# A four-layer graph network on one core: 46 instead of 42 target blocks of layer 3 from its table, and layer 0's table made first

## The chip, the core and the metric

The kernel runs on one core of a Trainium2 chip. The core has five engines that work side by side, each through its own queue in order: TensorE (PE; its weight loads, PEld, overlap its matmuls), VectorE (DVE), ScalarE (ACT), GpSimd (POOL) and SyncE (SP), which here only issues transfers. The metric is the time of the one core in microseconds (us), as the median of several runs.

## What is computed

There are 12,500 nodes of 128 features and 212,500 directed edges, sorted by target (a random graph in both directions, and a loop at each node). Four layers follow each other; each adds its result to x:

```
h = relu(layernorm(x));  x += L0(h)    # attention: Wh[src], 4 heads, softmax over a target's edges, gelu, layernorm
h = relu(layernorm(x));  x += L1(h)    # sum over edges of h[src] * edge_weight1, gelu, @W.T + b, gelu
h = relu(layernorm(x));  x += L2(h)    # h[src] mixed with 9 edge features, summed by target
h = relu(layernorm(x));  x += L3(h)    # mean of h[src] by target @Wl.T + b, + h@Wr.T, batch norm over nodes
```

In each layer the costly part is the same: fetch the row of each edge's source, and add the rows up by target.

## The kernel before

**Blocks and groups.** Nodes come in 98 blocks of 128 (`NB`), handled four at a time in 25 batches (`NBK`, `NK`). Edges come in 208 groups of 1,024 (`NG`, `GE`), eight slots of 128. As edges are sorted by target, a group's targets lie within a window of 128 nodes.

**Two ways to sum by target.** *By gather:* a group's source rows are fetched by eight indirect transfers that POOL issues (`gather`, line 661, and `gather_apart`, line 669), a one-hot matrix of the targets is made, and eight matmuls add the rows into the window, which DVE adds to the accumulator. *By table* (layers 1 and 3, `tabled1` and `tabled`): the layer's whole node table is held on chip (`tabS`). For each target block ("window", `NW` of them) the edges have been sorted by source block into 26 rows of 128 places (`NT`). A step takes one such row: four small matmuls pick the source rows out of `tabS` into `px` (lines 1200 and 1443), ACT copies and in layer 1 weights them, and one matmul scatters them to the window (`pw`, lines 1181 and 1429). What finds no place in its rows is gathered, one transfer for each window (`last`). Before the change blocks 56 to 97 (`W0_ = 56`, `NW = 42`) go by table in both layers, and the first `G0 = 121` groups by gather.

**Prologue.** The edges' targets and sources are loaded (`load_edges`, lines 128 to 138) and each group's base, relative targets (`rel`, stored again as `rel16`) and safety conditions worked out; small weights are loaded and transposed; then layer 0's table `tab0` (Wh and the source's part of the attention) and `sdt` (the target's part) are made in 25 batches (lines 917 to 952). Outside the layers' loops a list scheduler places the instructions on the engines by priority in the order of the source, as tiles and engines come free.

**Layer 0** (loop over `g`, lines 1093 to 1135, in the order written): loads for `g + 2`; the gathers and attention logits of `g` (`logits`, lines 992 to 1015); one-hot matrices on ACT (`hot`); every fourth group the softmax (`weights`, lines 1017 to 1063, scans on DVE); for group `g - 7` the messages (`spread_out`, line 1078, matmuls at 1082) and the addition to the accumulator (`add_up`, line 1086). 15 X buffers hold gathered rows. Beside this `Slots` (lines 750 to 916) sorts the edges of the 42 table blocks, three windows at a time (`quad`), mostly on DVE; its work is cut into steps: one `slots.step()` in each group and one more in every second (`slots.step(g % 2)`). A three takes 22 steps, so 14 threes take 308.

**Layer 3** (lines 1473 to 1566): group `g` is gathered into `xg` (28 buffers) while PE multiplies group `g - 1` into `pg` (line 1544, one PSUM buffer) and DVE reads `pg` of `g - 2` (lines 1536, 1537) and adds it up. From group 10 on, the table's steps are spread over the matmuls of the groups:

```
goal = total * (T * (g - first) + t + 1) // (T * (last_ - first + 1))
```

Finished batches go through `node3` (count, mean, two matrix products) and, at the end, `closing` (batch norm). Layer 1 is built likewise. Layer 2 goes by gather alone.

The functions that the change touches:

Of the kernel before, what the change touches and what calls it, by code (L numbers as in the profile page):

```python
# [14 lines left out]
F = mybir.dt.float32  # L15
# [11 lines left out]
P = 128  # L27
# [66 lines left out]
def gnn_kernel(ctx: ExitStack, tc, x, src, dst, ef16, ef9, ew, W0, We0, a0, lns, lnb, W1, b1,  # L94
# [11 lines left out]
    W0_ = NB * 56 // 98 // NBK * NBK  # L106
    NW = NB - W0_
    G0 = E * W0_ * P // (N * GE) + 2
# [88 lines left out]

    si = cst.tile([P, NG, T], I, name="si")
# [6 lines left out]
    early = ExitStack()  # L205
    tmp = early.enter_context(tc.tile_pool(name="acp", bufs=1))
    wslot = tmp.tile([P, NW, NT], F, name="wslot")
    bir = cst.tile([P, NG], I, name="bir")
    relx = cst.tile([P, GM, T], F, name="relx")
# [5 lines left out]
    NK = -(-NB // NBK)  # L215
# [5 lines left out]
    with tc.tile_pool(name="ed", bufs=1) as ep:  # L221
# [45 lines left out]
        last = base[:, G0 - GM : G0, None].to_broadcast([P, GM, T])  # L267
        vec.tensor_tensor(relx, rel[:, G0 - GM : G0, :], last, ALU.add)
        vec.tensor_scalar(relx, relx, W0_ * P - 0.5, 4.0 * P, op0=ALU.is_gt, op1=ALU.mult)
        vec.tensor_tensor(relx, relx, rel[:, G0 - GM : G0, :], ALU.add)  # L270
# [6 lines left out]
        vec.memset(least, 0.0)  # L277
        for k, g in enumerate(done):
            if g + 1 < NG:
                vec.memset(least[:, g + 1 :], float(min(NBK * P * (k + 1), N)))  # L280
        vec.memset(least[:, G0:], float(W0_ * P))
        for k, g in enumerate(done):
            if g + 1 >= G0 and g + 1 < NG:
                vec.memset(least[:, g + 1 :], float(min(NBK * P * (k + 1), N)))
# [3 lines left out]
        vec.memset(end, float(RW - W))  # L288
        for k, g in enumerate(done):
            if g + 6 < NG:  # L290
                vec.memset(end[:, g + 6 :], float(NBK * P * (k + 1) + RW - W))
# [27 lines left out]
        vec.tensor_scalar(many, red[:, 0, G0 - GM - 1 : G0 - GM], W0_ * P - 0.5, None, op0=ALU.is_gt)  # L319
        vec.scalar_tensor_tensor(worst, many, float(W), worst, op0=ALU.mult, op1=ALU.max)  # L320
# [17 lines left out]
    WE = cst.tile([P, P + 2 * H], F, name="WE")  # L338
# [3 lines left out]
    with tc.tile_pool(name="wt", bufs=2) as wp, tc.tile_pool(name="wtp", bufs=2, space=PSUM) as pp:  # L342
        for w, to in ((W0, WE[:, :P]), (W1, W1T), (Wl, WlT), (Wr, WrT)):
            wn = wp.tile([P, P], F, name="wn")
            nc.sync.dma_start(wn, w)
            wps = pp.tile([P, P], F, name="wps")
            pe.transpose(wps, wn, ident)
            vec.tensor_copy(to, wps)
            if w is W0:
                ab = wp.tile([P, 2 * H], F, name="ab", bufs=1)  # L350
                vec.memset(ab, 0.0)
                for h in range(H):
                    for s in range(2):
                        nc.sync.dma_start(ab[h * HD : (h + 1) * HD, s * H + h : s * H + h + 1],
                                          a0[h : h + 1, s * HD : (s + 1) * HD].rearrange("o d -> d o"))
                aps = pp.tile([P, 2 * H], F, name="aps", bufs=1)
                pe.matmul(aps, wn, ab, start=True, stop=True)
                vec.tensor_copy(WE[:, P:], aps)
# [67 lines left out]
    tab0 = dram.tile([N, P + H], F, name="tab0")  # L426
    sdt = dram.tile([AW, 3 * H], B16, name="sdt")
# [491 lines left out]
    WN = P + 2 * H  # L919
    with tc.tile_pool(name="p0", bufs=2) as sp, tc.tile_pool(name="p0p", bufs=2, space=PSUM) as pp:  # L920
        zs = sp.tile([P, 3 * H], B16, name="zs", bufs=1)
        vec.memset(zs, 0.0)
        for r in range(N, AW, P):
            n = min(P, AW - r)
            nc.sync.dma_start(sdt[r : r + n, :], zs[:n, :])
        for b0, nb in batches(4):
            xt = sp.tile([P, nb, D], F, name="xt")
            load_rows(xt, x, b0, nb)
            h = sp.tile([P, nb, D], F, name="h0")
            for _ in norm(sp, xt, nb, h):  # L930
                pass
            pt = pp.tile([P, nb, P], F, name="pt")
            for j in range(nb):
                pe.transpose(pt[:, j, :], h[:, j, :], ident)
            hT = sp.tile([P, nb, P], F, name="hT")
            act.copy(hT, pt)
            pw = pp.tile([P, 2, 512], F, name="pw")
            pwv = pw[:, :, : 2 * WN].rearrange("p a (c n) -> p a c n", n=WN)
            for j in range(nb):
                pe.matmul(pwv[:, j // 2, j % 2, :], hT[:, j, :], WE, start=True, stop=True)  # L940
            tt = sp.tile([P, nb, P + H], F, name="tt")
            sd = sp.tile([P, nb, H], F, name="sd")
            for a in range(0, nb, 2):
                act.copy(tt[:, a : a + 2, :], pwv[:, a // 2, : min(2, nb - a), : P + H])
                vec.tensor_copy(sd[:, a : a + 2, :], pwv[:, a // 2, : min(2, nb - a), P + H :])

            s3 = sp.tile([P, nb, 3, H], B16, name="s3")
            for k in range(3):
                vec.tensor_copy(s3[:, :, k, :], sd)
# [815 lines left out]
```

## Time and profile before

| | |
|---|---|
| median of 3 runs | 7448.18 us (7439.46 to 7453.02) |
| profiled execution: its own time, its span | 7429.66 us, 7427.8 us |
| mean granted TensorE clock | 0.789 of full |
| busy share of the span: PE, DVE, ACT, POOL | 68%, 71%, 38%, 69% |
| gathers on POOL: layers 0, 1, 2, 3 | 1,664, 968, 1,664, 968 |
| first and last gather of layer 0 | 231.9 and 2416.3 us |
| of layer 1 | 2524.9 and 3804.8 us |
| of layer 2 | 3900.5 and 5980.5 us |
| of layer 3 | 6016.7 and 7308.7 us |

The profile is of one execution. In its lines L661 is line 661 of the kernel before; a group of instructions is given as line, engine, operation, output<-input, count, then busy us and the mean ns of one, then the idle time of the engine just before them and what ended it ("issue": it waited for nothing that the profile shows). SPq is SP's transfer queue. A list of waits gives for each waiter and releaser the total us, the times and the longest one.

### The profile page before, as it was taken

Reading aid. Unit: us, or ns where it says so; the run is one execution under the profiler, and the core shown is the slowest. Engines: PE = TensorE matmul, PEld = TensorE weight load, DVE = VectorE, ACT = ScalarE, POOL = GpSimd, SP = SyncE. Lnnn points to the kernel's source line nnn. Section 1 sums busy time; section 2 is a strip of 40 time slices with the busy share of each in tenths; the row PEclk is TensorE's granted clock in tenths of the full one; section 3 lists DMA queues with packets and bytes.
Section 4 is the critical chain, followed back from the end, with each engine's and each line's share of the span. In section 5 each row is a group of like instructions: output and inputs, shape, how many; then the busy total and the mean of one; then the engine's idle time right before and its main releaser. Section 6 shows DMA issues by size and latency. Waiting matters only on the chain.

```text
span 7427.8 us, 119421 instructions
## 1 busy us (share of the span) xinstructions
PE 5056.1 (68%) x39957; PEld 3687.5 (50%) x39958; DVE 5283.1 (71%) x10506; ACT 2841.6 (38%) x7693; POOL 5145.2 (69%) x5372
## 2 busy tenths in 40 slices
PE   3344445444444499888987787778787758788787
PEld 2344444344444366555656777777777732222222
DVE  5678888888888445544448999999999944545454
ACT  1244444444444234434443333333333314444443
POOL 0577777777775377777737777777777767777772
PEclk8566666666666699999987888888888868888887
DMA  5444444444443433333322222222222244344333
GB/s 84 96 105 103 104 106 105 107 106 103 105 105 94 84 88 96 95 90 94 93 72 57 67 71 66 68 69 67 70 69 66 69 126 105 105 106 105 102 103 108
DMA packets 741279, 674.54 MB, mean 91 GB/s; under 512 B 341283, under 2 KB 629398, under 8 KB 740631
## 3 DMA queue, kind: packets, MB, share of 16 engines
q0 software_dynamic: 186624, 382.17, 21.4%
q1 hardware_dynamic: 554027, 284.63, 15.0%
q8 instruction: 316, 5.18, 0.3%
q14 instruction: 312, 2.56, 0.1%
HBM read 603.91 MB, written 63.28 MB: 90 GB/s over the span
## 4 chain that ended last, share of the span: by engine, by line
PE 26%; POOL 16%; DVE 10%; issue 9%; DMA 3%; ACT 1%; DVEq 1%; SPq 0%; POOLq 0%; ACTq 0%
POOL X L661 15%; PE pw L1181 5%; PE px L1200 5%; PE px L1443 4%; PE pw L1429 4%; PE pag L1275 3%; PE pg L1544 3%; DMA X<-htab,si 2%; DVE oh L680 1%; POOL X L669 1%; DVEq L692 1%; PE pag L1332 1%; DVE oh L676 1%; DVE f L1536 1%; DVE B L1314 1%
## 5 line engine op out<-in xcount | busy, mean ns | idle before, releaser
L661 POOL DMA_INDIRECT X<-tab,si x1664 | 1635.6, 983 | 531.0 <-issue 473.0
L661 POOL DMA_INDIRECT X<-htab,si x1664 | 1574.0, 946 | 533.7 <-issue 509.7
L669 POOL DMA_INDIRECT xg<-tab,si x968 | 919.7, 950 | 358.9 <-issue 127.3
L669 POOL DMA_INDIRECT X<-htab,si x968 | 937.1, 968 | 324.2 <-issue 83.8
L1082 PE MATMUL pag<-oh,msg 128*128 128x128 f32 x3328 | 670.5, 383 | 357.4 <-DVE msg L1078 328.7
L1082 PEld LDWEIGHTS pag<-oh,msg 128*128 128x128 f32 x3328 | 620.3, 288 | 373.7 <-DVE msg L1078 336.5
L1454 ACT CAST xb<-px 128x384 bf16<-128x384 f32 x1050 | 501.3, 478 | 737.4 <-PE px L1443 722.0
L1212 ACT ACTIVATE xs<-px,wslot 128x128 f32<-128x128 f32 x1050 | 382.6, 367 | 774.7 <-PE px L1200 698.2
L1332 PE MATMUL pag<-oh,A 128*128 128x128 f32 x3328 | 561.4, 341 | 0.0
L1544 PE MATMUL pg<-xg,oh 128*128 128x385 bf16 x968 | 370.9, 388 | 256.4 <-DVE f L1537 194.9
L1275 PE MATMUL pag<-oh,X 128*128 128x128 f32 x1936 | 432.6, 309 | 165.5 <-DVE acc L1268 121.6
L1332 PEld LDWEIGHTS pag<-oh,A 128*128 128x128 f32 x3328 | 543.5, 256 | 0.0
L1181 PE MATMUL pw<-ohb,xs 128*128 128x128 f32 x2100 | 541.3, 342 | 0.0
L1307 ACT ACTIVATE A<-X,ef 128x128 f32<-128x128 f32 x1664 | 509.9, 391 | 15.7 <-DMA X<-htab,si 15.4
L676 DVE TENSOR_TENSOR oh<-iop,rel 128x1024 f32<-128x1024 f32 (+1 forms) x321 | 388.7, 1211 | 163.2 <-PE pg L1544 162.7
L1200 PE MATMUL px<-tabS,oha 128*32 128x128 f32 x8652 | 488.1, 299 | 5.8 <-ACT xs L1212 5.8
L1071 ACT ACTIVATE oh<-iop,far 128x128 f32<-128x128 f32 x1664 | 451.6, 382 | 48.9 <-DVE ohj L879 38.7
L1181 PEld LDWEIGHTS pw<-ohb,xs 128*128 128x128 f32 x2100 | 334.4, 200 | 219.8 <-issue 218.0
L1334 ACT COPY R<-pag 128x256 f32<-128x256 f32 x208 | 77.4, 372 | 955.6 <-PE pag L1332 955.6
L1332 PE MATMUL pag<-oh,B 128*128 128x128 f32 x3328 | 437.8, 288 | 0.0
L1275 PEld LDWEIGHTS pag<-oh,X 128*128 128x128 f32 x1936 | 326.3, 212 | 206.6 <-DVE acc L1268 139.6
L1332 PEld LDWEIGHTS pag<-oh,B 128*128 128x128 f32 x3328 | 427.3, 208 | 0.0
(460 smaller groups left out, 10444.9 us busy)
## 6 DMA issues: line engine op xcount, KB each, us to landing
lob<-lo SPq DMA_DIRECT2D x252, 224.0 KB
rb<-rel SPq DMA_DIRECT2D x208, 256.0 KB
X<-htab,si POOLq DMA_INDIRECT x2632
X<-tab,si POOLq DMA_INDIRECT x1664
xtab<-xv SPq DMA_DIRECT2D x72, 256.0 KB
xv<-xtab SPq DMA_DIRECT2D x72, 256.0 KB
xg<-tab,si POOLq DMA_INDIRECT x968
lob<-lo SPq DMA_DIRECT2D x84, 160.0 KB
```

Of the source, the lines that this page charges most:

```text
L661: pool.indirect_dma_start(out=t[:, s, :], out_offset=None, in_=table[:, :], in_offset=bass.IndirectOffsetOnAxis(ap=idx[:, s : s + 1], axis=0))
L669: pool.indirect_dma_start(out=ts[-1][:, : table.shape[1]], out_offset=None, in_=table[:, :], in_offset=bass.IndirectOffsetOnAxis(ap=idx[:, ...
L676: vec.tensor_tensor(s, iop[:, None, :].to_broadcast([P, T, W]), r[:, :, None].to_broadcast([P, T, W]), ALU.is_equal)
L1071: act.activation(S[:, t, :], iop, AF.Abs, bias=far[:, t : t + 1])
L1082: pe.matmul(pag, msg[:, t, :], S[:, t, :], start=t == 0, stop=t == T - 1)
L1181: pe.matmul(pw, x, b, start=j == 0, stop=j == NT - 1)
L1200: pe.matmul(px[q * SL : (q + 1) * SL, :], a[:, jj * P + q * SL : jj * P + (q + 1) * SL], tabS[:, blk, :], start=True, stop=True)
L1275: pe.matmul(p, r[t], s[:, t, :], start=t == 0, stop=t == T - 1)
L1307: act.activation(A[:, t, :], X[:, t, :], AF.Copy, scale=e[:, t, 0:1])
L1332: pe.matmul(pag[: TPK[c] * HD, c, :], lhs, S[:, t, :], start=t == 0, stop=t == T - 1)
L1454: act.copy(x[:, : 3 * P], px)
L1544: pe.matmul(p, s[:, t, :], r[t], start=t == 0, stop=t == T - 1)
```

## The change

1. Layer 3's boundary `W0_` goes from block 56 to 52: 46 windows by table, and `G0` falls from 121 to 112 groups by gather. Layer 1 keeps 56 (`W1_`, `G1 = 121`) and starts its table at window `I1 = 4`.
2. `Slots` sorts 46 blocks, with `slots.step(g % 4 > 0)` in place of `slots.step(g % 2)`: 7 steps in four groups instead of 6.
3. Layer 0's table moves ahead of the edge preparation in the source, with x loaded eight batches ahead into nine buffers and three buffers for most other tiles. The normalization is folded into ACT's relu (bias and scale per row), the table rows are copied out of PSUM by DVE instead of ACT, and the target's part is kept for all blocks, split and stored once at the end.
4. The constants of the safety conditions (`least`, `end`) and the accumulator's first zeros are set by POOL instead of DVE. There are two sets of boundary targets: `relx` for layer 3, now bf16, and `relx1` for layer 1.

The diff, cut to its core:

```diff
-    W0_ = NB * 56 // 98 // NBK * NBK
-    NW = NB - W0_
-    G0 = E * W0_ * P // (N * GE) + 2
+    W0_, W1_ = (NB * b // 98 // NBK * NBK for b in (52, 56))
+    NW, I1 = NB - W0_, W1_ - W0_
+    G0, G1 = (E * b * P // (N * GE) + 2 for b in (W0_, W1_))
...
+    early, pre = ExitStack(), ExitStack()
+    tmp = early.enter_context(tc.tile_pool(name="acp", bufs=1))
+    sp, pp = (pre.enter_context(p) for p in (tc.tile_pool(name="p0", bufs=3),
+                                             tc.tile_pool(name="p0p", bufs=2, space=PSUM)))
+    xs0 = {}
+
+    def rows0(k):
+        if k < NK:
+            b0, nb = k * NBK, min(NBK, NB - k * NBK)
+            xs0[k] = sp.tile([P, nb, D], F, name="xt", bufs=9)
+            load_rows(xs0[k], x, b0, nb)
+
+    NK = -(-NB // NBK)
+    for k in range(8):
+        rows0(k)
...
+    sdall = sp.tile([P, NB, H], F, name="sdall", bufs=1)
+    for k in range(NK):
+        b0, nb = k * NBK, min(NBK, NB - k * NBK)
+        xt = xs0.pop(k)
...
+        for j in range(nb):
+            vec.bn_stats(st[:, j, :], xt[:, j, :])
+        for j in range(nb):
+            vec.bn_aggr(mv[:, j, :], st[:, j, :])
+        rs = sp.tile([P, nb], F, name="rs")
+        act.activation(rs, mv[:, :, 1], AF.Sqrt, bias=eps)
+        vec.reciprocal(rs, rs)
+        mr = sp.tile([P, nb], F, name="mr")
+        vec.scalar_tensor_tensor(mr, mv[:, :, 0], -1.0, rs, op0=ALU.mult, op1=ALU.mult)
+        h = sp.tile([P, nb, D], F, name="h0")
+        for j in range(nb):
+            act.activation(h[:, j, :], xt[:, j, :], AF.Relu, bias=mr[:, j : j + 1], scale=rs[:, j : j + 1])
+        pt = pp.tile([P, nb, P], F, name="pt")
+        for j in range(nb):
+            pe.transpose(pt[:, j, :], h[:, j, :], ident)
+        hT = sp.tile([P, nb, P], F, name="hT")
+        act.copy(hT, pt)
+        tt = sp.tile([P, nb, P + H], F, name="tt")
+        for a in range(0, nb, 2):
+            n = min(2, nb - a)
+            pw = pp.tile([P, 2, WN], F, name="pw")
+            for j in range(n):
+                pe.matmul(pw[:, j, :], hT[:, a + j, :], WE, start=True, stop=True)
+            vec.tensor_copy(tt[:, a : a + n, :], pw[:, :n, : P + H])
+            vec.tensor_copy(sdall[:, b0 + a : b0 + a + n, :], pw[:, :n, P + H :])
+        store_rows(tab0, tt, b0, nb, P + H)
+        rows0(k + 8)
...
+    s3 = sp.tile([P, NB, 3, H], B16, name="s3", bufs=1)
+    for k in range(3):
+        vec.tensor_copy(s3[:, :, k, :], sdall)
+        if k < 2:
+            vec.tensor_tensor(sdall, sdall, s3[:, :, k, :], ALU.subtract)
+    store_rows(sdt, s3.rearrange("p j k h -> p j (k h)"), 0, NB, 3 * H)
...
-    relx = cst.tile([P, GM, T], F, name="relx")
+    relx = cst.tile([P, GM, T], B16, name="relx")
+    relx1 = tmp.tile([P, GM, T], F, name="relx1")
...
-        last = base[:, G0 - GM : G0, None].to_broadcast([P, GM, T])
-        vec.tensor_tensor(relx, rel[:, G0 - GM : G0, :], last, ALU.add)
-        vec.tensor_scalar(relx, relx, W0_ * P - 0.5, 4.0 * P, op0=ALU.is_gt, op1=ALU.mult)
-        vec.tensor_tensor(relx, relx, rel[:, G0 - GM : G0, :], ALU.add)
+        for k, (t, gb, wb) in enumerate(((relx, G0, W0_), (relx1, G1, W1_))):
+            own = rel[:, gb - GM : gb, :]
+            far = ep.tile([P, GM, T], F, name=f"far{k}")
+            vec.tensor_tensor(far, own, base[:, gb - GM : gb, None].to_broadcast([P, GM, T]), ALU.add)
+            vec.tensor_scalar(far, far, wb * P - 0.5, 4.0 * P, op0=ALU.is_gt, op1=ALU.mult)
+            vec.tensor_tensor(t, far, own, ALU.add)
...
+        need = [max([0] + [min(NBK * P * (k + 1), N) for k, d in enumerate(done) if d < g] +
+                    [b * P for b, gb in ((W0_, G0), (W1_, G1)) if gb <= g]) for g in range(NG)]
+        for g in range(NG):
+            if g == 0 or need[g] != need[g - 1]:
+                pool.memset(least[:, g:], float(need[g]))
...
+        pool.memset(end, float(RW - W))
...
-    WN = P + 2 * H
-    with tc.tile_pool(name="p0", bufs=2) as sp, tc.tile_pool(name="p0p", bufs=2, space=PSUM) as pp:
...
-        for b0, nb in batches(4):
-            xt = sp.tile([P, nb, D], F, name="xt")
-            load_rows(xt, x, b0, nb)
-            h = sp.tile([P, nb, D], F, name="h0")
-            for _ in norm(sp, xt, nb, h):
-                pass
-            pt = pp.tile([P, nb, P], F, name="pt")
-            for j in range(nb):
-                pe.transpose(pt[:, j, :], h[:, j, :], ident)
-            hT = sp.tile([P, nb, P], F, name="hT")
-            act.copy(hT, pt)
-            pw = pp.tile([P, 2, 512], F, name="pw")
-            pwv = pw[:, :, : 2 * WN].rearrange("p a (c n) -> p a c n", n=WN)
-            for j in range(nb):
-                pe.matmul(pwv[:, j // 2, j % 2, :], hT[:, j, :], WE, start=True, stop=True)
-            tt = sp.tile([P, nb, P + H], F, name="tt")
-            sd = sp.tile([P, nb, H], F, name="sd")
-            for a in range(0, nb, 2):
-                act.copy(tt[:, a : a + 2, :], pwv[:, a // 2, : min(2, nb - a), : P + H])
-                vec.tensor_copy(sd[:, a : a + 2, :], pwv[:, a // 2, : min(2, nb - a), P + H :])
-
-            s3 = sp.tile([P, nb, 3, H], B16, name="s3")
-            for k in range(3):
-                vec.tensor_copy(s3[:, :, k, :], sd)
-                if k < 2:
-                    vec.tensor_tensor(sd, sd, s3[:, :, k, :], ALU.subtract)
-            store_rows(tab0, tt, b0, nb, P + H)
-            store_rows(sdt, s3.rearrange("p j k h -> p j (k h)"), b0, nb, 3 * H)
...
+    pre.close()
     acc.t = tmp.tile([P, RW + W], F, name="acc")
     H1 = H + 1
-    vec.memset(acc.t, 0.0)
+    pool.memset(acc.t, 0.0)
...
-                slots.step(g % 2)
+                slots.step(g % 4 > 0)
...
-        pieces = [(i, j, min(PT, NT - j)) for i in range(NW) for j in range(0, NT, PT)]
+        pieces = [(i, j, min(PT, NT - j)) for i in range(I1, NW) for j in range(0, NT, PT)]
...
-        first, last_ = 6, G0 - 1
-        total = NW * NT
+        first, last_ = 6, G1 - 1
+        total = (NW - I1) * NT
...
-                if g < G0:
+                if g < G1:
-                    S[g] = one_hot(sp, relx[:, g - G0 + GM, :] if g >= G0 - GM else rel[:, g, :], eww[:, g, :])
+                    S[g] = one_hot(sp, relx1[:, g - G1 + GM, :] if g >= G1 - GM else rel[:, g, :], eww[:, g, :])
...
```

## The prediction

> **What bounds the kernel now.** I read the page's slices first, then the busy time by stage (the stages' edges are the first and last gather of each layer), then, layer by layer, what the gather engine and the engines behind it wait for. A group is 1,024 edges; its rows come in by eight gathers on POOL.
>
> The page's slices (40 equal parts of the span, busy tenths):
>
> ```profile
> DVE  5678888888888445544448999999999944545454
> ...
> POOL 0577777777775377777737777777777767777772
> PEclk8566666666666699999987888888888868888887
> ```
>
> POOL stands at 7 nearly everywhere and never at 9. A gather is busy 0.94 us and is followed by 0.30 us of issue, so 7 tenths is a POOL that issues without a break, 1.25 us each. The stages:
>
> ```profile
> 0.00:99.90 99.90, 8.80 (x21) 3.97 (x22) 53.54 (x222) 0.02 (x1) 3.22 (x16) 1.00 0.62 61
> 99.90:231.90 132.00, 76.39 (x294) 59.79 (x294) 81.93 (x497) 50.32 (x125) 0.22 (x2) 0.58 0.45 101
> 231.90:2416.30 2184.40, 990.41 (x7220) 897.99 (x7220) 1824.80 (x3911) 913.39 (x2465) 1634.85 (x1664) 0.64 0.44 104
> 2524.90:3804.80 1279.90, 1129.88 (x12126) 753.39 (x12126) 613.53 (x1712) 500.38 (x1277) 972.68 (x1008) 0.90 0.36 94
> 3900.50:5980.50 2080.00, 1640.36 (x11822) 1541.48 (x11822) 1922.69 (x2489) 689.88 (x2367) 1573.28 (x1665) 0.86 0.26 67
> 6016.70:7308.70 1292.00, 1008.27 (x6891) 299.09 (x6891) 620.30 (x1246) 545.00 (x1139) 955.38 (x1010) 0.83 0.42 111
> ```
>
> Columns: stretch, length, then busy us of PE, PEld, DVE, ACT, POOL, the granted clock, DMA share, GB/s. The lines are edge preparation and constants, layer 0's table, and the gathers of layers 0 to 3. Layer 2 is 1,664 gathers x 1.25 = 2,080 us to the tenth: gathers set it. Layer 0 has as many and took 104 us longer; layer 3 has 968 plus 42 overflow gathers, 1,010 x 1.25 = 1,262, and took 30 us longer. So something else has a hand in layers 0 and 3, the two that the change loads.
>
> Layer 0, by the tile X:
>
> ```profile
> L661 POOL DMA_INDIRECT X<-tab,si x1664: 940/944/2173, 231.9 to 2416.3; - x185
> ...
> L1011 DVE TENSOR_TENSOR at<-at,X x208: 191/192/226, 244.0 to 2437.7; 128x32 f32<-128x32 f32 x104
> ```
>
> Taken group by group in the trace, group 0's logits (line 1011) start 2 us after its last gather, group 102's 38 us after, group 198's 74 us after: POOL advances 10.31 us a group, DVE 10.67. The lead ends only at the 15 X buffers, near the layer's end. DVE, not POOL, paces layer 0, though it is busy only 1,825 of 2,184 us; its idle time goes to short waits in its in-order queue:
>
> ```profile
> DVE f L1027 <- DMA d<-dpad: 82.1, 35, 8.8
> DVE acc L1086 <- PE pag L1082: 43.9, 32, 2.6
> ```
>
> Layer 3's costliest groups:
>
> ```profile
> L669 POOL DMA_INDIRECT xg<-tab,si x968 | 919.7, 950 | 358.9 <-issue 127.3 <-PE pg L1544 90.5 <-PE px L1443 79.4
> ...
> L1443 PE MATMUL px<-tabS,oha 128*32 128x384 bf16 x4326 | 421.2, 377 | 0.2
> L1429 PE MATMUL pw<-xb,ohb 128*128 128x385 bf16 x1050 | 395.0, 376 | 4.1 <-ACT xb L1454 3.8
> L1544 PE MATMUL pg<-xg,oh 128*128 128x385 bf16 x968 | 370.9, 388 | 256.4 <-DVE f L1537 194.9 <-DMA xg<-tab,si 50.5 <-DVE xo L1400 10.6
> ```
>
> Here POOL waits for PE. From group 10, where the table steps begin, to group 120 (6122 to 7336 us) PE takes 11.04 us a group: 8.93 of work and 2.11 of gaps, mostly the first pg of a group waiting for DVE to read the one pg bank (line 1537). POOL ran at 10.54 until the 28 xg buffers were used up, near group 50, and then at PE's pace. PE sets layer 3.
>
> **The change part by part.**
>
> *Layer 3, four blocks from gather to table.* Removed: 9 groups, 72 gathers (72 x 1.25 = 90 us of POOL, less 4 x 1.25 for new overflow gathers: 85). That is worth nothing while PE is the later. Added on PE: 4 windows x 26 steps = 104. In the timeline a step (four px and one pw) is issued every 0.55 us at full clock and every 0.87 at the lower one; at the stage's mean about 0.63, so 65 us; and four window ends at 1.5 (transposes and its wait on DVE): 6. Off PE: 72 pg at 0.22 = 16, nine groups' closing transposes 7, nine gaps of 1.7 = 15, one gathered node batch fewer, with its 3.35 us DVE reciprocal that stalls PE: 6. Net +27. A fuller PE may be granted more clock: 0.90 where it was busy 88% (layer 1), 0.83 here at 78%; a point or two on 1,030 us of work is up to -15. I take +20, bounds -15 and +45.
> The Trainium skill ("TensorE: Matmul & The Clock Gate", Part 1) says that the array runs at half clock after an idle window of about 3.4 us and at full clock after as long a busy one. By it the 1.7 us gaps would leave the clock alone and only the 14 long stalls (4.6 to 6 us) would drop it, and this term would stay near +20.
>
> *Layer 0, four more blocks sorted.* All on DVE, the pacing engine. Each window repeats twelve kinds of instruction, the two dearest being
>
> ```profile
> L884 DVE TENSOR_TENSOR load<-ohj,pq 128x2600 bf16<-128x2600 bf16 x42 | 119.7, 2851 | 0.0
> L876 DVE TENSOR_TENSOR ohr<-iop,r 128x2560 bf16<-128x2560 f32 x42 | 118.2, 2814 | 18.1 <-ACT oh L1071 18.1
> ```
>
> and together 14.4 us a window; what is issued once for three windows is 12.9. 46 windows are 15 threes and a single: 4 x 14.4 + 12.9 + about 8.5 = 79 us. The sort is now stepped 7 times in 4 groups where it was 6, so its 342 steps end near group 195 (308 ended near 205): denser, not hidden. Across the trace's groups a microsecond of sorting lengthens a group by 0.91 us (fitted with the position in the four-group cycle): 72. The first groups, where DVE still waits for gathers, absorb 6: +66. Bounds: +25 if the denser steps fill two thirds of the idle time before lines 1027 and 1086, +80 if none.
>
> *Prologue.* Before: the first gather at 231.9; the edge work ran to 99.9, then 25 table batches at 5.07 us, a chain PE to ACT (tt copy, relu) to PE in which no engine was full. The new form takes the tt copy off ACT (49 PSUM copies of 264 on DVE, about 0.43 each from the 0.29 of line 348 for 128: 21 us), folds the normalization into ACT's relu (line 451's 28.0 us leave DVE), and does the three-way split once (75 + 50 small instructions, 20.9 us, become five of about 0.5). DVE's busy time goes from 135.5 to about 110, with 8.3 us of memsets now on POOL, idle there. With edge work and table side by side the floor is that DVE sum: first gather at about 120. What keeps it from the floor is SP:
>
> ```profile
> 1.27 15.61 SPq L128 DMA_DIRECT2D si<-in_src_dram  x1
> ```
>
> The two index loads go in 32-byte pieces, 26,496 each, and held SP's queue until 31.5 us. Issued behind nine x loads (2.3 MB) and the weights, they would hold it until about 42, and the table's stores behind them; with three tt buffers three batches are done by then. Then 22 batches at about 3.3 us (DVE 2.6, ACT 2.4, PE 1.9 at full and 3.3 at half clock) end near 115, and the edge work that did not fit between, with its serial end (rel16 stores 13 us, weights 6, mixer 10), takes until about 150; 5 more to the first gather, as before. I take 157: -75. Bounds: -110 (DVE never idle) and -40 (edge work hardly overlaps).
> The Trainium skill ("DMA: Bandwidth & Descriptors", Queues, rings and completion order) says that descriptors are consumed in ring order on each DMA engine, which speaks against putting the stores behind the index loads; were it not so the first gather would come near 130.
>
> *The rest.* relx as bf16, relx1, and acc's memset on POOL: no waits seen at these places, nothing. Layer 1 keeps 42 windows and 121 groups, layer 2 is untouched: 0, and the tails of all layers likewise.
>
> **Sum.** -75 + 66 + 20 = +11, on the profiled execution 7429.66 us: 7441. That execution lies 18.5 us (0.25%) under the median of 7448.18, to which the forecast refers: 7448 + 11, say 7460.
>
> **The rivals.** (a) *Sorting hides in DVE's idle time* (faster). Place: layer 0's waits before lines 1027 and 1086, 82 and 44 us. If the denser steps use 40 us of them, layer 0 costs +25 and the whole is -30, 7418. For: these waits end by themselves while DVE does something else. Against: the 0.91 above. It decides from the point where layer 0 grows by under 40 us. (b) *POOL sets layer 3* (faster): with 10.54 us x 102 groups it would end 113 us earlier, 7326 in all. It needs PE under 10.54 us a group with 1.9 more steps in each. (c) *The table does not really come first* (slower): order in the source is not order on the engines (line 957's memset ran at 13.4 us). If index loads, edge chain and table still end one behind the other and the first gather comes at 195, the gain is 37: +49, 7497.
>
> **How the numbers follow.** Forecast 0.56, own range -30 to +55 (7418 to 7503); (a) 0.20, (b) 0.07, (c) 0.17. The three terms nearly cancel, so the sign is open. What a measurement of this kernel can tell from no change is about 0.2%, 15 us. Faster: 0.10 of the forecast's case, 0.15 of (a), 0.07 of (b): 0.32. Slower: 0.25 and 0.16 of (c), rounded up for the forecast's upper bounds: 0.44. Within: 0.24. The range leaves out (b) and the outer ends: 7385 to 7515.
>
> **What would show it.** First gather at 140 to 185 us; layer 0 from first to last gather 2,230 to 2,265 us with DVE lagging to the buffers' limit by group 170 and POOL waiting for msg (line 1078's counterpart); layer 1 1,280 and layer 2 2,080 us unchanged; layer 3 with 112 groups at about 12.2 us of PE. Wrong, if layer 0 keeps its 2,184 us, if layer 3's POOL is back at 1.25 us per gather, or if the first gather lies outside 120 to 195.

## The result, and the profile after

The changed kernel takes 7497.73 us (median of 4, 7490.26 to 7500.99) against 7443.82 (median of 4): ratio 1.0077, 95% interval 1.0064 to 1.009. It is slower, by 54 us or 0.8%. Its profiled execution has a span of 7487.8 us against 7427.8: 60 us to be found. The experiments below ran in four series, each with the kernel of before beside it: before took 7432.88 us in the series of e5 to e8 and 10,009 to 10,203 us in the other three, where the engines do about the same work (in layer 0 of the prologue alone VectorE is busy 1,790 us in e1 and 1,828 in e6) but wait much longer, so that times are compared inside a series only.

The page's slices of the kernel after:

```profile
POOL 1777776677665377777747777777777767666661
```

POOL's first digit is 1 now: the gathers begin inside the first slice. In slices 35 to 39, which lie in layer 3, POOL has gone from 7 to 6: it is held up more than before.

The stages, in the same columns as above (stretch, length, busy us of PE, PEld, DVE, ACT, POOL, clock, DMA share, GB/s):

```profile
0.00:125.00 125.00, 58.64 (x303) 44.94 (x304) 86.69 (x424) 58.66 (x150) 12.19 (x67) 0.78 1.02 149
125.00:171.20 46.20, 5.12 (x12) 2.11 (x12) 13.62 (x95) 0.00 (x0) 0.01 (x1) 0.50 0.61 17
171.20:2462.50 2291.30, 1061.17 (x7442) 959.62 (x7442) 1912.30 (x4078) 924.38 (x2490) 1632.01 (x1665) 0.62 0.42 99
2554.30:3833.40 1279.10, 1127.18 (x12181) 752.20 (x12184) 616.91 (x1727) 502.44 (x1282) 971.87 (x1009) 0.91 0.37 94
3923.90:6005.10 2081.20, 1640.95 (x11816) 1543.90 (x11817) 1923.34 (x2489) 689.44 (x2364) 1574.49 (x1664) 0.86 0.26 67
6039.40:7355.40 1316.00, 1030.67 (x7260) 310.89 (x7260) 621.80 (x1260) 590.40 (x1237) 890.92 (x941) 0.85 0.40 106
```

Edge preparation and table overlap in the first line; the second line is a tail of 46 us in which VectorE works for 13.6 us, the other engines hardly at all, and 17 GB/s flow. Then the gathers of the four layers. The account, from first and last gathers:

| stretch | before | after | difference | forecast |
|---|---|---|---|---|
| to the first gather | 231.9 | 171.2 | -60.7 | -75 |
| layer 0, first to last gather | 2184.4 | 2291.3 | +106.9 | |
| from there to layer 1's first gather | 108.6 | 91.8 | -16.8 | |
| layer 0 in all | 2293.0 | 2383.1 | +90.1 | +66 |
| layers 1 and 2, to layer 3's first gather | 3491.8 | 3485.1 | -6.7 | 0 |
| layer 3, first to last gather | 1292.0 | 1316.0 | +24.0 | |
| from there to the end | 119.1 | 132.4 | +13.3 | |
| layer 3 in all | 1411.1 | 1448.4 | +37.3 | +20 |

Layer 0 in the kernel after: the tile X, and POOL's and VectorE's waits from 171 to 2470 us (waiter, releaser: total us, times, longest):

```profile
L728 POOL DMA_INDIRECT X<-tab,si x1664: 938/944/2079, 171.2 to 2462.5; - x185
L1043 DVE TENSOR_TENSOR at<-at,X x208: 191/192/232, 183.9 to 2465.7; 128x32 f32<-128x32 f32 x104
```
```profile
POOL X L728 <- DVE msg L1110: 107.4, 34, 9.3
```
```profile
DVE f L1059 <- DMA d<-dpad: 66.3, 29, 9.2
DVE bI L860 <- DMA ss<-in_src_dram: 47.7, 12, 7.2
...
DVE acc L1118 <- PE pag L1114: 28.6, 25, 2.6
DVE relc L959 <- PE pq L956: 23.8, 23, 1.9
DVE ohb L892 <- PE pq L890: 20.7, 18, 2.6
```

The same waits in the kernel before, where the sort's lines are L793, L892 and L825:

```profile
POOL X L661 <- DVE msg L1078: 8.0, 10, 5.3
```
```profile
DVE bI L793 <- DMA ss<-in_src_dram: 24.4, 6, 5.3
DVE relc L892 <- PE pq L889: 8.8, 11, 1.3
DVE ohb L825 <- PE pq L823: 3.3, 12, 1.5
```

POOL now waits 107 us for `msg`, that is for a free X buffer; before it was 8. And the short waits in which sorting might have hidden fell by only 15 us each (82 to 66, 44 to 29), while the sort's own waits grew: for its loads (L860) from 24 to 48 us, and for PE's sums from 9 to 24 (L959) and from 3 to 21 (L892). The two dearest instructions of the sort, four windows more at the old price:

```profile
L951 DVE TENSOR_TENSOR load<-ohj,pq 128x2600 bf16<-128x2600 bf16 x46 | 131.3, 2854 | 0.0
L943 DVE TENSOR_TENSOR ohr<-iop,r 128x2560 bf16<-128x2560 f32 x46 | 129.5, 2815 | 10.1 <-ACT oh L1103 10.1
```

Layer 3's groups of instructions after:

```profile
L736 POOL DMA_INDIRECT xg<-tab,si x896 | 852.0, 951 | 423.5 <-PE pg L1576 166.9 <-issue 83.5 <-PE px L1475 81.6
L1475 PE MATMUL px<-tabS,oha 128*32 128x384 bf16 x4620 | 442.4, 372 | 0.3
L1461 PE MATMUL pw<-xb,ohb 128*128 128x385 bf16 x1120 | 415.4, 371 | 5.4 <-ACT xb L1486 5.2
L1576 PE MATMUL pg<-xg,oh 128*128 128x385 bf16 x870 | 329.2, 382 | 245.5 <-DVE f L1569 184.1 <-DMA xg<-tab,si 50.5 <-DVE xo L1432 10.7
```

Nine groups fewer, and PE still waits 184 us for VectorE's read of the `pg` bank (195 before); POOL's wait for `pg` has grown from 91 to 167 us.

### The profile page after: what moved, and what is told of

It reads as the page before. It is cut to its first block, busy times and chain, and to the rows that moved or that the text cites. A ratio compares the mean times of both kernels' runs of the same rounds, so it can differ in the third digit from the quotient of the medians.

```text
span 7487.8 us, 120661 instructions
## 1 busy us (share of the span) xinstructions
PE 5124.5 (68%) x40541; PEld 3740.9 (50%) x40542; DVE 5326.2 (71%) x10447; ACT 2902.8 (39%) x7825; POOL 5087.3 (68%) x5354
## 4 chain that ended last, share of the span: by engine, by line
PE 27%; POOL 18%; DVE 12%; issue 11%; DMA 4%; ACT 1%; DVEq 1%; SPq 1%; POOLq 0%; ACTq 0%
POOL X L728 16%; PE pw L1213 5%; PE px L1232 5%; PE px L1475 4%; PE pw L1461 4%; PE pag L1307 3%; PE pg L1576 2%; DMA X<-htab,si 2%; DVE oh L747 1%; PE pag L1364 1%; POOL X L736 1%; DVEq L759 1%; DMA X<-tab,si 1%; DVE oh L743 1%; DVE f L1568 1%
## 5 line engine op out<-in xcount | busy, mean ns | idle before, releaser
L736 POOL DMA_INDIRECT xg<-tab,si x896 | 852.0, 951 | 423.5 <-PE pg L1576 166.9
L1114 PE MATMUL pag<-oh,msg 128*128 128x128 f32 x3328 | 703.6, 397 | 360.6 <-DVE msg L1110 333.2
L1114 PEld LDWEIGHTS pag<-oh,msg 128*128 128x128 f32 x3328 | 651.2, 300 | 376.9 <-DVE msg L1110 339.9
L1486 ACT CAST xb<-px 128x384 bf16<-128x384 f32 x1150 | 548.1, 478 | 719.1 <-PE px L1475 695.9
L1307 PE MATMUL pag<-oh,X 128*128 128x128 f32 x1936 | 428.2, 307 | 169.2 <-DVE acc L1300 121.7
L1576 PE MATMUL pg<-xg,oh 128*128 128x385 bf16 x896 | 339.0, 383 | 248.9 <-DVE f L1569 187.5
L1475 PE MATMUL px<-tabS,oha 128*32 128x384 bf16 x4738 | 453.8, 372 | 0.3
```

The source lines that it names most:

```text
L736: pool.indirect_dma_start(out=ts[-1][:, : table.shape[1]], out_offset=None, in_=table[:, :], in_offset=bass.IndirectOffsetOnAxis(ap=idx[:, ...
L1114: pe.matmul(pag, msg[:, t, :], S[:, t, :], start=t == 0, stop=t == T - 1)
L1307: pe.matmul(p, r[t], s[:, t, :], start=t == 0, stop=t == T - 1)
L1475: pe.matmul(px[q * SL : (q + 1) * SL, :], a[:, jj * P + q * SL : jj * P + (q + 1) * SL], tabS[:, blk, :], start=True, stop=True)
L1486: act.copy(x[:, : 3 * P], px)
L1576: pe.matmul(p, s[:, t, :], r[t], start=t == 0, stop=t == T - 1)
```

## The experiments

The prologue takes the same time in all four series: the first gather comes at 166.7 to 170.4 us in every run below.

The stages, from first and last gathers as above:

| run | median us | ratio to before, interval | first gather | layer 0 | to layer 1 | layer 1 | layer 2 | layer 3 | to the end |
|---|---|---|---|---|---|---|---|---|---|
| e5, after again | 7486.18 | 1.007 (1.0055 to 1.0085) | 169.6 | 2292.7 | 89.5 | 1277.1 | 2080.5 | 1322.8 | 130.5 |
| e6, prologue alone | 7366.12 | 0.9915 (0.9898 to 0.9931) | 168.0 | 2184.2 | 107.6 | 1277.3 | 2078.8 | 1297.9 | 121.2 |
| e7, pg read early | 7320.1 | 0.9845 (0.9831 to 0.9859) | 169.2 | 2287.1 | 91.3 | 1280.3 | 2079.9 | 1179.9 | 96.3 |
| e8, sdt by ACT | 7491.94 | 1.0078 (1.0063 to 1.0094) | 166.7 | 2289.5 | 89.7 | 1276.4 | 2080.3 | 1322.9 | 129.9 |
| e1, prologue alone | 9943.23 | 0.9934 (0.9918 to 0.9951) | 168.6 | 3015.4 | 160.8 | 1637.7 | 2830.3 | 1701.6 | 121.9 |
| e2, sorted, not used | 9931.82 | 0.9916 (0.9898 to 0.9933) | 169.6 | 3037.2 | 135.8 | 1630.3 | 2836.3 | 1702.8 | 114.8 |
| e3, pg read early | 9730.84 | 0.9714 (0.9696 to 0.9731) | 169.0 | 3042.2 | 134.3 | 1637.7 | 2845.3 | 1489.9 | 124.0 |
| e4, sdt moved in the source | 9879.5 | 0.9857 (0.9839 to 0.9876) | 169.6 | 3054.1 | 134.3 | 1624.0 | 2832.6 | 1630.3 | 129.8 |
| e9, early read, 46 in layer 1 too | 9665.27 | 0.9651 (0.9638 to 0.9664) | 170.3 | 3053.6 | 133.8 | 1566.8 | 2830.0 | 1490.1 | 127.1 |
| e10, early read, 42 blocks | 9793.37 | 0.9784 (0.9769 to 0.9799) | 167.7 | 3029.4 | 163.0 | 1634.1 | 2835.1 | 1544.4 | 114.7 |
| e11, copies on ACT | 9918.44 | 0.9901 (0.9886 to 0.9916) | 170.4 | 3086.2 | 133.9 | 1633.5 | 2832.3 | 1629.3 | 127.3 |
| e12, four together | 9915.49 | 0.9714 (0.97 to 0.9727) | 167.3 | 3133.6 | 137.2 | 1594.4 | 2947.1 | 1502.0 | 124.9 |

### The prologue alone (e1, e6), and the change again (e5)

```diff
-    W0_, W1_ = (NB * b // 98 // NBK * NBK for b in (52, 56))
+    W0_, W1_ = (NB * b // 98 // NBK * NBK for b in (56, 56))
-                slots.step(g % 4 > 0)
+                slots.step(g % 2)
```

> The new prologue alone: sorting, layer 1 and layer 3 keep 42 blocks as before. Theory (the prologue's gain is real and whole, the four blocks are a loss in two layers): first gather at 171 us as in the changed kernel, layer 0 from first to last gather 2,184 to 2,195 us and its tail as before, layer 3 1,292 us; about 7443.8 - 61 - 5 = 7378 us. Rival 1 (the earlier first gather is paid back in layer 0, because what was moved or the new buffers slow it, and the sorting is not what costs): layer 0 grows by 40 us or more with no block added, 7420 to 7445 us. Rival 2 (part of layer 3's growth comes with the other edits, relx as bf16 or the pools): layer 3 above 1,305 us with 42 blocks.

> The changed kernel itself, as the reference of this series, because the first four runs came from a chip on which the kernel of before takes 10,014 us (there every instruction lasts as long as on the first chip, but all engines idle longer between groups). Expected: where before takes 7,440 us, a ratio of 1.006 to 1.010 as on the first chip; where it takes 10,000 us, 0.985 to 0.988, since the run with sdt's store moved in the source turned out to be issued in the same order as the changed kernel and gave 0.9857.

> The new prologue alone, 42 blocks everywhere. Theory (the prologue's gain is real and whole, the four blocks lose in layers 0 and 3): where before takes 7,440 us, first gather at 171, layer 0 2,184 to 2,195 us, layer 3 1,292 us, 7378 us in all, ratio 0.990 to 0.993. Rival (the earlier first gather is paid back in layer 0): layer 0 40 us longer with no block added, ratio 0.997 or more. On the slow chip it gave 0.9934.

e6 is 66.8 us faster than before, what the earlier first gather is worth (63.9) and 3 more; nothing is paid back in layer 0. Put back the four blocks (e5) and 120 us are lost. In the profiled executions, which differ by 129 us, 90.4 of them are in layer 0 with its tail (108.5 - 18.1) and 34.2 in layer 3 with its tail (24.9 + 9.3). Layer 0 of e6, then of e5:

```profile
168.00:2352.20 2184.20, 980.76 (x7220) 887.48 (x7220) 1828.05 (x3911) 914.62 (x2465) 1631.92 (x1665) 0.64 0.42 104
```
```profile
169.60:2462.30 2292.70, 1053.41 (x7442) 953.87 (x7442) 1914.88 (x4078) 924.77 (x2490) 1634.33 (x1664) 0.63 0.40 99
```

VectorE is busy 86.8 us more, and the layer is 108.5 longer between its gathers, 90.4 with its tail. VectorE's idle time did not shrink at all (356 and 378 us). So layer 0 charges four blocks in full, their work, their denser steps and the waits of these together; no run tells the three apart. In layer 3, e6 has 1297.9 us with the new `relx` and 42 blocks: 6 us over the profiled before, so nearly all of layer 3's loss is the blocks'.

### Sorting 46 blocks and using 42 of them in layer 3 (e2)

The edit gives layer 3 the boundary of layer 1 (`W1_`, `G1`, `I1`); cut to its core:

```diff
...
-        for i in range(NW):
+        for i in range(I1, NW):
...
-            first, last_ = 10, G0 - 1
-            total = NW * NT
+            first, last_ = 10, G1 - 1
+            total = (NW - I1) * NT
```

> The changed kernel with 46 blocks sorted in layer 0, of which layer 3 uses only 42, as layer 1 does: what layer 3's four blocks cost is taken away, what their sorting costs stays. Theory (layer 3 is paced by PE, so a block costs more there than its gathers give back): layer 3 back at 1,292 us and a tail of 119, layer 0 at 2,291 as in the changed kernel; 7497.7 - 37 = 7460 us, slower than before by 0.2%. Rival (layer 3's growth is not the blocks but where their sorted lists lie or the other edits): layer 3 stays above 1,310 us, 7490 to 7500 us.

This kernel leaves out one step: the four blocks that are gathered again are not divided by their edge counts (one batch of `node3`, whose VectorE reciprocal is 3.35 us). It ran where before takes 10,014 us. Against e1, layer 0 with its tail did not grow (3173.0 and 3176.2), and layer 3 is the same (1702.8 and 1701.6): sorting cost nothing there, and layer 3's difference from e4 comes with the blocks that it takes from the table. Of the theory's sizes it says nothing, because in that series VectorE's own work does not pace layer 0: in e4, which has the changed kernel's instructions (see below), it is busy 1,891 of 3,054 us. Its longest waits in layer 0 of e4:

```profile
DVE ohb L891 <- remote: 223.1, 25, 49.3
DVE relc L958 <- remote: 192.9, 31, 13.9
DVE at L1042 <- issue: 100.5, 13, 23.9
```

In idle time of that size four blocks can hide, which is argued and not shown; and there the change is faster, 0.9857. What makes these waits stays open.

### Reading the pg bank first in layer 3 (e3, e7)

```diff
+                    h = g - 2
+                    if 0 <= h < G0:
+                        flat3[h] = sp.tile([P, P + 1], F, name="f3")
+                        ...
                     if g % 8 == 0 and (g + 16) * W < W0_ * P:
...
-                    h = g - 2
-                    if 0 <= h < G0:
-                        flat3[h] = sp.tile([P, P + 1], F, name="f3")
-                        ...
```

> The changed kernel; in layer 3 VectorE reads the finished pg bank (reduce and copy to f) at the head of a group, ahead of the memset, the one-hot and the two adds of that group, which took 1.2 + 0.27 + 0.28 us in front of it. Theory (what bounds layer 3 is PE's wait of 1.7 us a group for that read, because there is one pg bank): the wait on f (187 us) falls to under 70 us, and layer 3 to what POOL allows, 942 gathers x 1.25 = 1,178, say 1,190 to 1,215 us instead of 1,316; 7498 - 110 = 7388 us. Rival 1 (PE's own work bounds, and the wait only moves, to px, pw or the nodes): layer 3 falls by under 40 us, 7460 us or more. Rival 2 (VectorE now waits for PE at the head of its queue, and the table's one-hots come late): layer 3 no shorter, 7498 us or more.

> The changed kernel with VectorE's read of the pg bank in layer 3 at the head of the group. Theory (layer 3 is bounded by PE's wait of 1.7 us a group for that read): where before takes 7,440 us, layer 3 1,190 to 1,215 us instead of 1,316 and the whole 7385 to 7400, ratio 0.992 to 0.995. Rival (PE's own work bounds layer 3): over 1,280 us, ratio above 1.003. On the slow chip layer 3 fell from 1,630 to 1,490 us.

e7 is 166 us faster than the change as it stands (7320.1 and 7486.18) and 1.55% faster than before. That is below the 7385 to 7400 us expected: layer 3 gave 143 us, and its tail, which was not counted, 34. In e3's series the same edit took layer 3 from 1630.3 (e4) to 1489.9 us. Layer 3 of e7, and its groups of instructions up to 7,200 us:

```profile
6039.00:7220.00 1181.00, 1001.34 (x7438) 315.24 (x7438) 627.72 (x1310) 606.17 (x1270) 890.95 (x939) 0.89 0.44 118
```
```profile
L736 POOL DMA_INDIRECT xg<-tab,si x878 | 837.1, 953 | 301.4 <-PE px L1475 72.5 <-issue 71.9 <-PE pg L1576 45.1
...
L1475 PE MATMUL px<-tabS,oha 128*32 128x384 bf16 x4639 | 422.4, 353 | 0.5
...
L1576 PE MATMUL pg<-xg,oh 128*128 128x385 bf16 x873 | 314.5, 361 | 131.9 <-DMA xg<-tab,si 89.1 <-DVE f L1557 41.4 <-DVE acc L1559 0.2
```

The wait on f went from 184 to 41 us, and PE now waits for gathered rows instead. First to last gather took 1179.9 us, and 942 gathers x 1.25 are 1,177.5: POOL sets layer 3, and its tail shrinks by 34 us because PE no longer lags behind the gathers. The waits show where the time sat. VectorE's, in layer 3 of the kernel after and then of e7:

```profile
DVE oh L743 <- PE pg L1576: 138.3, 51, 8.3
```
```profile
DVE f L1556 <- PE pg L1576: 149.7, 54, 8.2
```

VectorE waits for the same matmuls in both. In the kernel after it then makes the one-hot of the next group (1.21 us) and two additions (0.27 and 0.28) before it frees the one `pg` bank; in e7 it frees it at once. The clock gains as well: 0.85 to 0.89, px from 372 to 353 ns. Four stretches of the kernel after, one behind the other:

```profile
6139.88:6146.70 6.82, 5.11 (x46) 1.61 (x42) 3.69 (x7) 3.13 (x7) 5.21 (x6) 1.00 0.32 86
6146.71:6150.11 3.40, 3.40 (x22) 0.79 (x21) 0.44 (x1) 1.64 (x4) 2.58 (x3) 0.50 0.55 143
6150.12:6156.94 6.82, 5.11 (x43) 1.60 (x39) 3.45 (x7) 3.35 (x7) 4.99 (x7) 1.00 0.35 99
6156.95:6160.35 3.40, 3.40 (x21) 0.80 (x20) 1.16 (x3) 1.43 (x3) 2.76 (x3) 0.50 0.50 136
```

In 6.82 us at full clock PE (first column after the length) is idle for 1.71 us, the wait for f, and the next 3.4 us are granted half. The Trainium skill ("TensorE: Matmul & The Clock Gate", Part 1) puts the step down to half clock at an idle window of about 3.4 us. From 100 us after the first gather to the last one, PE's gaps came to 228 us in the kernel after, 49 of them in ten gaps over 3.4 us, and to 121 us in e7, 21 of them in five. The clock stood at half for some 308 us of that stretch in the kernel after and 151 in e7, mostly with no gap of that length near, as in the rows above. So here half clock does not need a gap of 3.4 us: stalls of 1.7 us cost it too.

### sdt's store: moved in the source, issued by another engine, held back (e4, e8)

e4 moves one line, e8 replaces it:

```diff
-    store_rows(sdt, s3.rearrange("p j k h -> p j (k h)"), 0, NB, 3 * H)
...
+    store_rows(sdt, s3.rearrange("p j k h -> p j (k h)"), 0, NB, 3 * H)
     pre.close()
```
```diff
-    store_rows(sdt, s3.rearrange("p j k h -> p j (k h)"), 0, NB, 3 * H)
+    for b, n, r in rows(0, NB):
+        act.dma_start(sdt[b * P : b * P + (n - 1) * P + r, :].rearrange("(j p) d -> p j d", p=r),
+                      s3[:r, b : b + n].rearrange("p j k h -> p j (k h)"))
```

> The changed kernel with the one store of sdt (held SP for 24 us at 117 us) moved behind the rel16 stores, the weights and the mixer, to the end of the prologue. Theory (the prologue missed its 157 us because that store stood in front of the 13 rel16 stores on SP): rel16 goes out from about 124 us, the first gather comes at 148 to 156 us instead of 171, and the whole gets shorter by the same 15 to 23 us, 7478 us. Rival (the 24 us are then waited for by layer 0's first loads on the same queue, so nothing of the earlier first gather is left at group 20): 7495 to 7500 us.

> The changed kernel with the one store of sdt issued by ScalarE's queue, which has nothing to do then, instead of SP's. Theory (the first gather is late because that store holds SP's queue 22 to 24 us ahead of the rel16 stores): rel16 goes out from about 124 us, first gather at 146 to 154 us instead of 169 to 171; the whole 15 to 23 us shorter than the changed kernel. Rival (the small pieces load the DMA engines themselves, whichever queue they come from): the rel16 stores end no earlier than 150 us and the first gather stays at 165 or later.

The question is the 46 us tail of the prologue. In the timeline of the kernel after, SP's queue (start, us, line, transfer):

```profile
116.62 23.91 SPq L151 DMA_DIRECT2D sdt<-s  x2
140.63 13.03 SPq L413 DMA_DIRECT2D rel<-rl  x13
155.02 0.33 SPq L424 DMA_DIRECT2D wn<-in_L_gnn_W_dram  x1
```

The store goes in 12,500 pieces of 24 bytes, by the trace's packets. e4's timeline:

```profile
116.51 22.01 SPq L151 DMA_DIRECT2D sdt<-s  x2
138.62 13.64 SPq L412 DMA_DIRECT2D rel<-rl  x13
```

Nothing moved: outside the hand-ordered blocks the place in the source is not the place in the queue, and on every engine e4 has the changed kernel's instructions in the changed kernel's order, but for two of VectorE's in layer 3 that changed places. So it serves as the changed kernel's time in its series, 0.9857: there the change is 1.4% faster. e8's timeline:

```profile
115.88 22.89 ACTq L273 DMA_DIRECT2D sdt<-s  x2
123.08 26.09 SPq L415 DMA_DIRECT2D rel<-rl  x13
```

From ScalarE's queue the store takes as long, and SP's 13 stores, free to start at 123, now take 26 us instead of 13: the third waited until 137.6 for the first to land, when the other queue's store was nearly done. The theory falls and the rival holds: what is short is not SP's queue but what carries out the transfers. The first gather came 3 us earlier than in e5, and the whole was not faster. The Trainium skill ("DMA: Bandwidth & Descriptors", Queues, rings and completion order) says that each DMA engine takes turns between the queues' rings by packets; the row here is a store of 128 rows that took some 14 us to land beside another queue's small pieces, so taking turns did not bring it through early.

### 46 blocks in layer 1 too, and 42 with the early read (e9, e10)

Both are e7's kernel with one line changed, (52, 52) and (56, 56) in place of (52, 56), e10 with the old stepping as well.

> The changed kernel with the early read of pg in layer 3, and layer 1 too taking 46 blocks from its table (112 groups gathered instead of 121). What PE's share in layer 1 says: POOL's floor falls from 1,262 to (896 + 46) x 1.25 = 1,178 us, but PE, busy 1,129 of 1,277 us with 42 blocks, gets 104 steps more at about 0.77 and nine groups less at 2.85, +54, so about 1,183 busy. Theory (layer 1 turns from gathers to PE): 1,220 to 1,260 us instead of 1,280, the whole 7,260 to 7,300, ratio 0.977 to 0.982. Rival (POOL still sets layer 1, PE hides): 1,180 us, 7,220 in all, ratio 0.971. Second rival (a third wait like that of layer 3 comes up, on DVE's add before the next pag): layer 1 1,275 or longer, ratio 0.984 or more.

> The new prologue with 42 blocks everywhere and the early read of pg in layer 3. Theory (with that read early, POOL sets layer 3 at 1.25 us a gather, so a block moved to the table is worth its gathers, 85 us for four, and its sorting in layer 0 costs about 105 less the shorter tail 17, 90): layer 3 1,262 us instead of 1,298, its tail 95 to 120, layer 0 2,184; the whole 7,305 to 7,330, as good as the same with 46 blocks (7,320), ratio 0.982 to 0.987. Rival (sorting costs less than the gathers give back once PE no longer waits): 7,345 or more, ratio 0.988 or more.

Both ran where before takes 10,009 us, so the sizes expected were not tried. Beside e3 (0.9714, another series, where before took 10,013.71 instead of 10,009.31 us): layer 1 with 46 blocks is 71 us shorter (1566.8 and 1637.7) and e9 has the lowest ratio of all, 0.9651; with 42 blocks e10 is slower, 0.9784, its layer 3 54 us longer. Whether layer 1 gains where before takes 7,433 us stays open, as does the tie that was expected of e10, and so whether four more blocks pay at all there once `pg` is read early. By stages of e6, an estimate only: e6 with a layer 3 of 1,010 gathers x 1.25 = 1,262 would come to 7,330 before any gain in its tail, beside e7's 7,320.

### Copies of the sort on ScalarE (e11), and four edits together (e12)

```diff
-                vec.tensor_copy(load[:, :, 5 * NT], ob[:, k, :])
+                act.copy(load[:, :, 5 * NT], ob[:, k, :])
...
-                vec.tensor_scalar(relc[:, i, :], ps[:, NT : 2 * NT], -1.0, None, op0=ALU.add)
-                vec.tensor_copy(lof[:, k, :], ps[:, :NT])
+                act.copy(lof[:, k, :], ps[:, :NT])
+                act.activation(relc[:, i, :], ps[:, NT : 2 * NT], AF.Copy, bias=-1.0)
...
-            vec.tensor_copy(lot, pl)
+            act.copy(lot, pl)
```

> The changed kernel with four copies of the sorting (the overflow column of load, lof, relc, lot) on ScalarE instead of VectorE: 46 x (0.215 + 0.177 + 0.175) + 16 x 0.274 = 30.5 us less work for VectorE in layer 0. Theory (VectorE paces layer 0 and a microsecond of sorting costs a microsecond or a little more): layer 0 from 2,291 to about 2,259 us, the whole 7,455, ratio 1.002 to 1.004. Rival (what costs is the number of dependent steps and their waits, not the work): VectorE waits for ScalarE instead, layer 0 shorter by under 10 us, ratio 1.006 or more.

> Four edits on the changed kernel, each readable in a stage of its own: pg read early in layer 3; 46 blocks in layer 1 too; three copies of the sorting (load's overflow column, relc, lot) on ScalarE, placed so that VectorE waits for none of them; sdt's store held behind the rel16 stores and the weights by an order dependency. In a series in which before takes 7,440 us. Layer 3: 1,180 us as with the early read alone. Layer 1: PE has 1,183 us of work and POOL a floor of 1,178, so 1,220 to 1,260 instead of 1,280 if PE sets it; 1,275 or more if a wait like that of layer 3 does. Prologue: rel16 stores from about 124 us, first gather at 148 to 156 instead of 170, but the first sdw load still comes behind the store, at about 168 instead of 173, so only some 5 us of it are left at the end of layer 0. Layer 0: 46 x (0.215 + 0.177) + 16 x 0.274 = 22.4 us less for VectorE; if a microsecond of sorting costs a microsecond, its last gather comes at about 2,462 - 5 - 23 = 2,434 us; if steps and waits are what costs, at 2,455 or later. In all about 7,250 us, ratio 0.972 to 0.979. In a series in which before takes 10,010 us the first readings do not apply, and the ratio should be 0.962 to 0.967.

e12 keeps `lof` on VectorE, and holds the sdt store by

```diff
+        tc.add_manual_dep(put.ins, last_w.ins.name, NOSYNC, reason="order")
```

e11 ran where before takes 10,009 us, e12 where it takes 10,203. e11's layer 0 is 33 us longer than that of e9, which has the change's layer 0 and ran in the same series, and a wait that its edit made is VectorE's longest between 500 and 2,000 us:

```profile
DVE wslot L961 <- ACT relc L960: 117.5, 18, 14.0
```

There the added waits outweigh the work saved. The question of the expectation, whether the work of sorting costs or its steps and waits, stays open where before takes 7,433 us: e5 and e6 change both at once. e12's ratio of 0.9714 misses the 0.962 to 0.967 that was expected of it where before takes 10,010 us; in its series no other kernel but before ran, so its layers are not compared. Its prologue can be read:

```profile
123.17 12.96 SPq L412 DMA_DIRECT2D rel<-rl  x13
140.32 22.16 SPq L986 DMA_DIRECT2D sdt<-s  x2
166.49 0.06 DVE L999 MEMSET z<- 128x4 f32 x1 [14.44 <-DMA sdt<-s]
```

Now the 13 stores of `rel16` are out at 136 and the last weight matrix (`mixer`) is done by 152, and still the first gather comes at 167.3: the first tiles of layer 0 take the memory of `s3`, so VectorE, and behind it POOL, waits 14.4 us for the store to land. At each of the three places tried, the 22 us of that store lie on the path.

## Why the prediction was right or wrong

**The sign and the range held; the sum did not.** The forecast's working gave +11 us, the profiled executions differ by 60. The recorded range holds 7497.73 near its upper end, and slower had the largest chance, 0.44. That the sign came out is luck in good part: by its own account +11 us lay inside the 15 us that it could not tell from no change. All three terms were missed on the same side: by 14 (prologue), 24 (layer 0) and 17 (layer 3), less 7 for the other layers: 49 of 49.

**Prologue, -75 forecast, -60.7 measured.** The mechanism was right: index loads in the way, table stores waiting behind them (three of them took 14.9 us behind one load and 17.1 behind the other, elsewhere 0.4 each), a serial end after 125 us. VectorE's work even fell further than was said, to 100 us up to the first gather. The step that failed is the folding of the three-way split: it was priced as VectorE work saved, and its one store was not priced at all, though the prediction names SP's queue as what keeps the prologue from its floor. Before, the same pieces went in 25 stores between the table's batches, each holding SP's queue for 0.5 us at most; as one store they hold the transfers for 22 to 24 us with the rel16 stores behind them (e8, e12). That this is where the 14 us went is an estimate, as no run is without the store: less its last wait of 14.4 us, e12's first gather would come at 153 us, against 157 forecast.

**Layer 0, +66 forecast, +90 measured.** The work was sized well: 79 us forecast, 86.8 more busy time measured in e5 over e6. The step that failed is the factor 0.91 and the 6 us absorbed at the start. VectorE's idle time did not shrink: what the waits of the other steps lost (31 us) the denser sort put back with waits of its own (L860, L959 and L892: 56 us more), so the full price and a little more was charged. That the fit across groups misled because it was made at the old density is argued, not shown. The lag reached the buffers' limit, and POOL's wait for `msg`, 107 us, is the sign that was named; but it began at group 93 and not near 170, and the layer's 2,291 us lie above the 2,230 to 2,265 that were named with it.

**Layer 3, +20 forecast, +37.3 measured.** PE's pace was foretold at 12.2 us a group and came at 12.25 (11.03 before, both from group 10 to the last read of `pg`), so PE does set it, and this part grew by 24 us. Within it the term of the nine gaps that were to vanish with nine groups (15 us) failed: PE's gaps came to 226 us before and 228 after, over the same stretch; that the sum came near all the same is luck in part, as the work came cheaper than forecast, at a clock of 0.85 instead of 0.83. The second step that failed is the tail, put at nothing: from the last read of `pg` to the end it is 82.3 us before and 94.8 after (84.0 in e6, 92.9 in e5). With 46 blocks the last nodes' statistics come some 8.5 us later behind that read; no run tells why. Of the 14 long stalls that the prediction counts, the trace of before has seven (4.6 to 6.1 us), and gaps of 1.7 us do not leave the clock alone, as the rows at e7 show. And the stall for the one `pg` bank was found and named, but taken as given. e7 shows that it was the bound: without it the same table gives 1179.9 us.

**The rivals.** (a), sorting hides in idle time, is refuted where before takes 7,433 us (e5 and e6); where it takes 10,014 us, layer 0 did not grow (e2). (b), POOL sets layer 3, is false of the change, and true of it with one read moved (e7). It named PE under 10.54 us a group as the point of decision; in e7 a group takes 10.6 us, hardly more than the 10.5 that 942 gathers at 1.25 over 112 groups allow, and layer 3 is 112 us shorter than before, the 113 that the rival named. (c), the table does not come first, named a time, 7497, that was hit for another reason: the first gather came at 171, not 195.

**Layers 1 and 2** stayed where they were said to stay, 1,279 and 2,081 us.

## What to carry to other kernels

Where two parts of a change pull apart, price and run them apart: here the prologue alone was worth 0.85%, and the blocks took back nearly twice that. Before moving work onto an engine that waits for a bank, look at what stands between that wait's end and the instruction that frees the bank; putting the freeing read first was worth 166 us, more than twice the new prologue. And when stores are gathered into one, ask where in time its pieces now fall and what is queued behind them, not only which instructions are saved.

## What the runs showed of the hardware

- A store of 12,500 pieces of 24 bytes held SP's queue for 21.3 to 23.9 us and ScalarE's for 22.9, and with it the other queue's 13 stores took 26.1 us instead of 13.0; an index load of 26,496 pieces of 32 bytes took 15.6 us.
- Less idle time between PE's matmuls went with a higher granted clock in layer 3: gaps of 228 and 121 us, a clock of 0.85 and 0.89, the same matmul at 372 and 353 ns.
- Half clock came after PE had been idle for 1.71 of 6.82 us, with no gap near 3.4 us (rows at e7).
